# A state-space convolution block: loads of A moved to SP's queue, in-projection moved beside the first convolution, first scan's signs copied from PSUM

## The chip, the cores and the metric

The kernel runs on one core of one Trainium2 chip. The core has five engines with a queue each: TensorE (PE, matrix products into PSUM), VectorE (DVE), ScalarE (ACT), GpSimd (POOL) and SyncE (SP, which here only issues DMAs). DMAs can be issued from SP's queue and from ScalarE's. The metric is the time of one launch in microseconds of the device, the median of several runs, less is better.

## What is computed

The input x has 4 images of 64 x 64 pixels with 96 channels. Layer 0 is a binarised state-space block, layer 1 an attention without softmax and a feed-forward network. What the change touches is all in layer 0:

```python
x = x + conv_block(group_norm(x))
# conv_block, for each image:
xz = sign(x) @ (s_in * sign(W_in - mean)).T + b_in          # in-projection, 96 -> 2 * 192
xp, z = split(xz)
t = conv3x3(sign(xp + move0), scale * sign(conv_W))         # 192 -> 192 channels
t = prelu(t + conv_b + rp_b0) + rp_b1 + xp
xs = silu(t)                                                # in 4 directions: rows, columns, both reversed
dt_r, B, C = split(sign(xs) @ sign(Wl).T * sl + bl)         # 6 + 16 + 16 per direction
delta = softplus(sign(dt_r) @ sign(Wd).T * sd + bd + dt_bias)
A = -exp(A_logs)                                            # 4 x 192 x 16
h[l] = exp(delta[l] * A) * h[l-1] + delta[l] * xs[l] * B[l] # scan along 4096 positions
y[l] = sum_n h[l] * C[l] + D * xs[l]
y = layer_norm(sum over directions(y)) * silu(z)
out = sign(y) @ sign(W_out).T * s_out + b_out
```

Group norm before a sign needs only the mean, so the kernel sums the columns of x and adds the negative group mean before the sign.

## The kernel before

The work falls into a **head** and a long **scan loop**. The scan loop (`Scans.run`) goes through 1536 pieces (4 images, 4 directions, 4 chunks of 1024 positions, 6 groups of 32 channels, 4 quarters of the 16 states; 32 channels by 4 states fill 128 rows). Each piece takes an exponential on ScalarE (`decay`), a product on GpSimd (`inject`), a scan and, in part, a product with C on VectorE, and a reduction on PE. Beside it, a generator `back` brings the later images' preparations and the earlier images' epilogues, one step a piece. The order of instructions is written by hand: generators are advanced in turn by `interleave`, and every engine's queue takes its instructions in the order in which the program wrote them. `Later` holds back stores for some turns and then issues them on SP's queue.

The head prepares image 0 and all constants. `run` interleaves two generators:

- `weights()` (`made`). Up to its first `yield` it issues every load of a weight on SP's queue (L199 to L240), and on ScalarE's queue `pvd` (L241), `sbR` (L245 to L247) and the 24 loads of A (`anm`, L251: 32 rows of 16 single floats each). Then it takes the signs of `w_in` (L259) and transposes them. Its later steps make the convolution's weights and their scales (L265 to L270), the weights of the x projection (L290 to L303), of the delta projection (`wdz`, `wdy`, L314 to L329), then `dbias`, `dsum`, the exponential and negation of A (L336, L337), and many small constants up to L373. It has 22 steps.
- `prologue(c, 0, c.xts)` (`first`). It sums the columns of x on PE (L514, four steps), turns the sums into group means (L521 to L534, three steps), transposes x and takes the signs (`xfin`, eight steps; it also stores x plus the output bias, `xb`). Then comes the in-projection: for both halves h of the channels and all eight q of 512 pixels, two matmuls `px` and `pz` (L562), the sign of px into the padded image `tpad` (L564) and the sign of pz into `sz` (L569), which is stored to DRAM. `alone` is true for this image only.

Then `first` runs the convolution in 16 parts (h, q). A part is 18 matmuls (L616) into one half of the two-bank PSUM tile `cv2`, then v on VectorE (L653) and r on ScalarE (L656) from it, and a matmul `cz` (L658). While the next part's matmuls run in four steps s, the rest of this part is done: two VectorE operations at s = 0, `sign` and an exponential at s = 1, logarithm and exponential at s = 2, the product u at s = 3. The small working tiles come from a pool of eight (`f32`). Part n reads rows of `tpad` that the projections q = n and n + 1 of both halves wrote.

Then the signs are turned into pairs (L685, L690), multiplied (L737), and the six delta inputs of each direction are stored (`sgd`), loaded (`g`, L756), transposed through PE (L761), copied to `gt` (L766), stored (`gTd`, L767) and loaded twice by `load_signs` (L1161, L1162) into the tile `gT`: once at rows 0 to 47, once at rows 64 to 111 and shifted by 16 columns. `gT` feeds the delta matmuls of `prepare` (L1202). The first scan's direction is `KORD[0]` = 1.

```python
made, first = c.weights(), prologue(c, 0, c.xts)
lanes = [made, first]
while (0, 1) not in c.ready:
    interleave(lanes)
    c.later.tick()
```

Of the kernel before, what the change touches and what calls it, by code (L numbers as in the profile page):

```python
# [25 lines left out]
CH = 1024  # L26
# [27 lines left out]
def hybrid_kernel(ctx: ExitStack, tc: tile.TileContext, a: dict, out: bass.AP):  # L54
# [103 lines left out]
    def weights():  # L158
# [89 lines left out]
        for g in range(NG):  # L248
            src = a["al"][32 * (g % 4) : 32 * (g % 4) + 32, g // 4].rearrange("d k (q j) -> j d (k q)", j=4)
            for j in range(4):  # L250
                nc.scalar.dma_start(anm[j::4, g, :], src[j])  # L251
        for t in gTs + [wdz]:
# [82 lines left out]
        nc.vector.tensor_reduce(dsum, pv[:, :, DSK : DSK + NK], AX.X, ALU.add)  # L335
        nc.scalar.activation(anm, anm, AF.Exp)  # L336
        nc.vector.tensor_scalar(anm, anm, -1.0, None, ALU.mult)  # L337
        nc.vector.tensor_reduce(sum4, ident.rearrange("p (d j) -> p d j", j=4), AX.X, ALU.add)
# [94 lines left out]
def run(c):  # L433

    made, first = c.weights(), prologue(c, 0, c.xts)
    lanes = [made, first]
    while (0, 1) not in c.ready:
        interleave(lanes)
        c.later.tick()
# [40 lines left out]
def prologue(c, b, xts=None):  # L480
# [11 lines left out]
    with tc.tile_pool(name=f"xg_{b}", bufs=1) as xgp:  # L492
# [3 lines left out]
        with tc.tile_pool(name=f"cv_{b}", bufs=1) as cvp:  # L496
# [58 lines left out]
            for h in range(2):  # L555
                nc.gpsimd.memset(tflat[h].bitcast(F32), 0.0)
            for h in range(2):
                for q in range(NQ8):
                    cols = slice(512 * q, 512 * q + 512)
                    px, pz = bank(f"ix{h}{q}", 0)[0:96], bank(f"iz{h}{q}", 1)[0:96]  # L560
                    for ps, c0 in ((px, 96 * h), (pz, DN + 96 * h)):
                        nc.tensor.matmul(ps, c.winT[:, c0 : c0 + 96], xsT[:, cols], start=True, stop=True)  # L562
                    yield
                    nc.scalar.activation(  # L564
                        tpad[h][:, 1 + 8 * q : 9 + 8 * q, 1 : 1 + IW], px.rearrange("p (h w) -> p h w", w=IW),
                        AF.Sign, scale=pv[:, h, S_X : S_X + 1], bias=c.sbias[:, h : h + 1], saturate=False,
                    )
                    sz = f32(f"sz{h}{q}").bitcast(BF16)[0:96, 0:512]
                    nc.scalar.activation(  # L569
                        sz, pz, AF.Sign, scale=pv[:, h, S_Z : S_Z + 1], bias=pv[:, h, B_Z : B_Z + 1]  # L570
                    )
                    c.later.store(c.szd[b][h][:, cols], sz)

# [5 lines left out]
            prev = turned = None  # L579
            two = c.p.dA.tile([128, CH], F32, name=f"cv2_{b}", tag="dA") if alone else None  # L580
            utp = sub.enter_context(tc.tile_pool(name=f"ut_{b}", bufs=1))
# [23 lines left out]
            for n, part in enumerate(parts + [None]):  # L605
                if part:
                    h, q = part
                    nm = f"{h}{q}"
                    at = 512 * (n % 2)
                    ps = (two[:, at : at + 512] if alone else bank("cv" + nm, 0))[0:96]  # L610
                for s in range(4 if alone else 5):
                    if part:
                        per = 5 if alone else 4
                        for j, t in taps[per * s : min(18, per * s + per)]:
                            dy, dx = divmod(t, 3)
                            nc.tensor.matmul(  # L616
                                ps, c.cw[:, j, t, 96 * h : 96 * h + 96],
                                tpad[j][:, 8 * q + dy : 8 * q + dy + 8, dx : dx + IW],
                                start=(j == 0 and t == 0), stop=(j == 1 and t == 8),
                            )  # L620
                    if s == 0 and turned:
                        by_columns(*turned)
                        turned = None
# [46 lines left out]
        with tc.tile_pool(name=f"rw_{b}", bufs=1) as rw:  # L670
# [4 lines left out]
            tbg, sgg = (t.rearrange("p (g r) -> p g r", r=64) for t in (tbc, sgn))  # L675
            g2 = rw.tile([128, 2, 320], F8, name=f"g_{b}", tag="g")
            gw = g2.bitcast(F32)
            for o in (1, 0):
# [74 lines left out]
                if o:  # L753
                    nc.gpsimd.memset(gw[:, :, 48:80], 0.0)
                for x, k in enumerate((o, o + 2)):
                    nc.sync.dma_start(gw[:, x, 0:48], c.sgd[b][k].rearrange("(p f) -> p f", p=128))  # L756
                    yield
                    yield
                    gp = bank(f"gp{k}", k // 2).rearrange("p (s f) -> p s f", s=4)
                    for s in range(4):  # L760
                        nc.tensor.matmul(  # L761
                            gp[:, s, :], g2[:, x, 48 * s : 48 * s + 128], c.ident8, start=True, stop=True
                        )
                    yield
                    t = rw.tile([48, 4, 32], F32, name=f"gt_{b}_{k}", tag="gt", bufs=2)
# [362 lines left out]
class Scans:  # L1128
# [6 lines left out]
    def __init__(self, c):  # L1135
# [9 lines left out]
        self.late, self.cys = None, {}  # L1145
        self.us, self.gs, self.at, self.loaded, self.sums = {}, {}, -1, set(), {}

# [213 lines left out]
    def run(self, back):  # L1361
# [4 lines left out]
        for x in range(3):  # L1366
# [5 lines left out]
            )  # L1372
        interleave(lanes)
        for q in range(NQ):
            self.load_bc(0, self.bt, 0, 0, 0, q)
# [125 lines left out]
```

## Time and profile before

| what | us |
|---|---|
| median of 3 runs (5527.49 to 5539.79) | 5532.96 |
| profiled execution, own time | 5528.8 |
| its span, first to last instruction | 5527.0 |
| busy: VectorE | 5025.5 (91%) |
| busy: GpSimd | 4975.1 (90%) |
| busy: ScalarE | 3568.5 (65%) |
| busy: PE, matmuls | 3478.7 (63%) |
| first in-projection matmul (ix) | at 60.14 |
| first convolution matmul | at 84.13 |
| first delta matmul | at 233.01 |
| first injection on GpSimd | at 259.4 |
| first scan on VectorE | at 269.6 |
| mean granted clock of PE | 0.71 of full speed |

Times "at" count from the span's start. Lines of the profile that follow name an engine, a line of the kernel, an operation, and the tiles written and read. A queue such as "SPq" shows the issue of DMAs, not their running. In square brackets stands how long the engine had been idle before, and what released it. In a line of a timeline, several like instructions are merged, "x18" for example.

### The profile page before, as it was taken

How to read it: one execution, taken by the hardware profiler on the slowest of the kernel's cores; microseconds unless marked ns; L12 is line 12 of the kernel's file. 1: busy time of each engine (PE TensorE's matmuls, PEld its weight loads, DVE VectorE, ACT ScalarE, POOL GpSimd, SP SyncE). 2: the span in 40 equal slices, each digit the busy share in tenths (PEclk: the TensorE clock that was granted, in tenths of full speed). 3: DMA queues.
4: the chain of work that ended last, by engine and by line, in shares of the span. 5: the costliest groups of instructions: out<-in, count | busy, mean ns of one | idle time of the engine just before them, and what ended most of it. 6: DMA issues, size and time to landing. Idle time of an engine off the chain costs nothing. (4 is left out here: it accounts for less than half of the span.)

```text
span 5527.0 us, 62184 instructions
## 1 busy us (share of the span) xinstructions
PE 3478.7 (63%) x20133; PEld 1371.3 (25%) x20133; DVE 5025.5 (91%) x3198; ACT 3568.5 (65%) x5568; POOL 4975.1 (90%) x2255
## 2 busy tenths in 40 slices
PE   6456765467645776657665677664677664445677
PEld 2222222122222232222222232221232221111223
DVE  3299999999999999999999999999999999999984
ACT  4467766677666667777666666776556775555554
POOL 2199999899999999999999999999999999999981
PEclk8666776678777776767876777765787565666777
DMA  4455765767666666676765666667666566666652
GB/s 80 120 191 187 211 204 189 237 220 211 200 192 207 197 199 207 195 237 212 223 191 184 206 205 195 198 208 229 201 214 194 179 194 199 213 202 190 204 157 60
DMA packets 613243, 1069.92 MB, mean 194 GB/s; under 512 B 225083, under 2 KB 343924, under 8 KB 611124
## 3 DMA queue, kind: packets, MB, share of 16 engines
q1 hardware_dynamic: 599428, 1065.88, 62.0%
q8 instruction: 158, 2.59, 0.2%
q10 hardware_dynamic: 13488, 0.07, 0.1%
q14 instruction: 169, 1.38, 0.1%
HBM read 833.20 MB, written 229.38 MB: 192 GB/s over the span
## 5 line engine op out<-in xcount | busy, mean ns | idle before, releaser
L404 POOL TENSOR_TENSOR w<-dl,bc 128x1024 f32<-128x1024 f32 x1536 | 3578.8, 2356 | 158.7 <-PE yp L1340 69.6
L1267 ACT ACTIVATE dA<-dl,anm 128x1024 f32<-128x1024 f32 x1536 | 1714.6, 1116 | 495.5 <-DVE w L404 282.7
L404 DVE TENSOR_TENSOR_SCAN dA<-dA,cy,w 128x1024 f32<-128x1024 f32 x711 | 1665.8, 2343 | 98.7 <-ACT dA L1267 94.1
L1340 PE MATMUL yp<-w,sum 128*32 128x256 f32 x12288 | 1289.5, 515 | 401.5 <-POOL w L404 260.0
L404 POOL TENSOR_TENSOR w<-h,bc 128x1024 f32<-128x1024 f32 x587 | 1381.1, 2353 | 114.4 <-DVE h L404 104.2
L404 DVE TENSOR_TENSOR w<-dA,bc 128x1024 f32<-128x1024 f32 x949 | 1162.4, 1225 | 48.7 <-issue 0.9
L404 DVE TENSOR_TENSOR_SCAN h<-dA,cy,w 128x1024 f32<-128x1024 f32 x441 | 1031.6, 2340 | 8.6 <-ACT dA L1267 8.5
L1340 PEld LDWEIGHTS yp<-w,sum 128*32 128x32 f32 x12288 | 316.3, 129 | 1487.4 <-issue 710.4
L1309 ACT COPY cy<-dA 128x1 f32<-128x1 f32 x715 | 112.2, 157 | 747.8 <-DVE w L404 746.2
L404 DVE TENSOR_TENSOR_SCAN dA<-dA,w 128x1024 f32<-128x1024 f32 x238 | 543.3, 2283 | 29.1 <-ACT dA L1267 21.6
L616 PE MATMUL cv<-tp,cw 96*96 96x512 fp8e5 x1152 | 364.4, 452 | 46.2 <-ACT r L656 42.0
L404 DVE TENSOR_TENSOR_SCAN h<-dA,w 128x1024 f32<-128x1024 f32 x146 | 332.5, 2278 | 10.5 <-ACT dA L1267 9.1
L1202 PE MATMUL dps<-gT,wdz 128*128 128x64 fp8e5 x1000 | 113.7, 313 | 339.4 <-ACT ys L1354 310.1
L1215 PE MATMUL dps<-sp,ident 128*128 128x512 f32 x376 | 279.7, 834 | 47.0 <-ACT dps L1211 46.7
L1345 PE MATMUL yp<-ya,back 128*128 128x256 f32 x576 | 239.3, 537 | 1.6 <-DMA ya<-y 1.1
L616 PEld LDWEIGHTS <-cw 96*96 96x96 fp8e5 x1152 | 153.5, 144 | 234.1 <-issue 182.0
L1202 PEld LDWEIGHTS <-wdz 128*128 128x128 fp8e5 x1024 | 95.1, 152 | 427.3 <-issue 395.1
L1202 PE MATMUL dps<-gT,wdy 128*128 128x64 fp8e5 x504 | 59.3, 320 | 204.1 <-ACT ys L1354 202.0
L1309 ACT COPY cy<-h 128x1 f32<-128x1 f32 x437 | 81.4, 186 | 147.5 <-DVE h L404 146.4
L1207 ACT ACTIVATE pd<-dps,dbias,pvd 128x512 f32<-128x512 f32 x188 | 143.2, 761 | 22.6 <-PE dps L1202 22.6
L878 PE MATMUL yc<-eys,mean 96*96 96x512 f32 x240 | 139.2, 734 | 29.2 <-DVE vks L404 13.6
L1345 PEld LDWEIGHTS yp<-ya,back 128*128 128x128 f32 x576 | 123.8, 248 | 130.2 <-issue 93.3
(290 smaller groups left out, 4221.1 us busy)
## 6 DMA issues: line engine op xcount, KB each, us to landing
dl<-dld SPq DMA_DIRECT2D x768, 512.0 KB
bc<-bcd SPq DMA_DIRECT2D x512, 512.0 KB
dld<-pd SPq DMA_DIRECT2D x125, 512.0 KB
yd<-ys SPq DMA_DIRECT2D x768, 64.0 KB
dld<-pd SPq DMA_DIRECT2D x126, 256.0 KB
ya<-yd SPq DMA_DIRECT2D x192, 128.0 KB
pu<-ud SPq DMA_DIRECT2D x32, 512.0 KB
pu<-utd SPq DMA_DIRECT2D x30, 512.0 KB
```

The costliest lines, as they stand in the source:

```text
L404: return getattr(self.eng, name)(out, *args, **kw)
L616: nc.tensor.matmul(ps, c.cw[:, j, t, 96 * h : 96 * h + 96], tpad[j][:, 8 * q + dy : 8 * q + dy + 8, dx : dx + IW], start=(j == 0 and t == ...
L878: self.c.nc.tensor.matmul(ps, w, x, start=(i == 0), stop=(i == len(pairs) - 1))
L1202: nc.tensor.matmul(pv[:, s], wd[:, k, s], gT[:, :, c0 : c0 + 16], start=(s == 0), stop=(s == 7))
L1207: nc.scalar.activation(d[:, 0], ps, AF.Abs, scale=sc, bias=bi)
L1215: nc.tensor.matmul(ps, c.ident, t, start=False, stop=True, skip_group_check=True)
L1267: c.nc.scalar.activation(t, self.dlt[i // NQ][0], AF.Exp, scale=c.anm[:, g, NQ * KORD[e] + q : NQ * KORD[e] + q + 1])
L1309: self.c.nc.scalar.copy(self.carries[g, q], h[:, CH - 1 : CH])
L1340: c.nc.tensor.matmul(y[32 * x : 32 * x + 32, g % 2, :], c.sum4, prod[:, 256 * x : 256 * x + 256], start=(q == 0), stop=(q == NQ - 1 and no ...
L1345: c.nc.tensor.matmul(y[:, g % 2, :], w, src, start=False, stop=(n == len(more) - 1))
```

## The change

1. The 24 loads of A go from ScalarE's queue to SP's. Exponential and negation of A move from `weights()` into `Scans.run`, behind the first round of delta matmuls.
2. `run` advances `made` by one step and `first` by six (column sums and group means), before it interleaves the two.
3. For image 0, the in-projection becomes a list of 16 small generators `project(h, q)`, ordered by q and then h. Four of them run before the convolution. The other twelve run in its parts 0 to 5: matmuls at s = 0 and s = 2, the two signs at s = 1 and s = 3, in each case ahead of the part's other ScalarE work of that step. px and pz now share a second two-bank tile, and `sz` takes the pool `h` of two tiles instead of the pool of eight. The other images do what they did.
4. The tile `g` gets zeros on both sides of its data. For the first direction of image 0, the transposition is done twice, at two offsets, and the two results are copied from PSUM straight into the rows of `gT`. Store and loads of that direction are left out, and `Scans` starts with this tile entered in `gs`.

```diff
--- before.py
+++ after.py
@@ -248,7 +248,7 @@
         for g in range(NG):
             src = a["al"][32 * (g % 4) : 32 * (g % 4) + 32, g // 4].rearrange("d k (q j) -> j d (k q)", j=4)
             for j in range(4):
-                nc.scalar.dma_start(anm[j::4, g, :], src[j])
+                nc.sync.dma_start(anm[j::4, g, :], src[j])
         for t in gTs + [wdz]:
             nc.gpsimd.memset(t.bitcast(F32), 0.0)
 
@@ -333,8 +333,6 @@
                 yield
         nc.vector.tensor_tensor(dbias, pvd[:, :, NK : 2 * NK], pvd[:, :, 2 * NK :], ALU.add)
         nc.vector.tensor_reduce(dsum, pv[:, :, DSK : DSK + NK], AX.X, ALU.add)
-        nc.scalar.activation(anm, anm, AF.Exp)
-        nc.vector.tensor_scalar(anm, anm, -1.0, None, ALU.mult)
         nc.vector.tensor_reduce(sum4, ident.rearrange("p (d j) -> p d j", j=4), AX.X, ALU.add)
         yield
 
@@ -434,6 +432,9 @@
 
     made, first = c.weights(), prologue(c, 0, c.xts)
     lanes = [made, first]
+    next(made)
+    for _ in range(6):
+        next(first)
     while (0, 1) not in c.ready:
         interleave(lanes)
         c.later.tick()
@@ -554,22 +555,41 @@
             nc.gpsimd.memset(xgw[64:128, 1], 0.0)
             for h in range(2):
                 nc.gpsimd.memset(tflat[h].bitcast(F32), 0.0)
-            for h in range(2):
-                for q in range(NQ8):
-                    cols = slice(512 * q, 512 * q + 512)
+            two = [c.p.dA.tile([128, CH], F32, name=f"cv{i}_{b}", tag="dA") for i in range(2)] if alone else None
+
+            def project(h, q):
+
+                cols = slice(512 * q, 512 * q + 512)
+                if alone:
+                    px, pz = two[1][0:96, 0:512], two[1][0:96, 512:CH]
+                else:
                     px, pz = bank(f"ix{h}{q}", 0)[0:96], bank(f"iz{h}{q}", 1)[0:96]
-                    for ps, c0 in ((px, 96 * h), (pz, DN + 96 * h)):
-                        nc.tensor.matmul(ps, c.winT[:, c0 : c0 + 96], xsT[:, cols], start=True, stop=True)
+                for ps, c0 in ((px, 96 * h), (pz, DN + 96 * h)):
+                    nc.tensor.matmul(ps, c.winT[:, c0 : c0 + 96], xsT[:, cols], start=True, stop=True)
+                yield
+                nc.scalar.activation(
+                    tpad[h][:, 1 + 8 * q : 9 + 8 * q, 1 : 1 + IW], px.rearrange("p (h w) -> p h w", w=IW),
+                    AF.Sign, scale=pv[:, h, S_X : S_X + 1], bias=c.sbias[:, h : h + 1], saturate=False,
+                )
+                sz = c.p.h.tile([128, CH], F32, name=f"sz{h}{q}_{b}", tag="h") if alone else f32(f"sz{h}{q}")
+                sz = sz[0:96, 0:256].bitcast(BF16)
+                nc.scalar.activation(
+                    sz, pz, AF.Sign, scale=pv[:, h, S_Z : S_Z + 1], bias=pv[:, h, B_Z : B_Z + 1]
+                )
+                c.later.store(c.szd[b][h][:, cols], sz)
+
+            if alone:
+
+                ahead = [project(h, q) for q in range(NQ8) for h in range(2)]
+                for g in ahead[:4]:
+                    next(g)
                     yield
-                    nc.scalar.activation(
-                        tpad[h][:, 1 + 8 * q : 9 + 8 * q, 1 : 1 + IW], px.rearrange("p (h w) -> p h w", w=IW),
-                        AF.Sign, scale=pv[:, h, S_X : S_X + 1], bias=c.sbias[:, h : h + 1], saturate=False,
-                    )
-                    sz = f32(f"sz{h}{q}").bitcast(BF16)[0:96, 0:512]
-                    nc.scalar.activation(
-                        sz, pz, AF.Sign, scale=pv[:, h, S_Z : S_Z + 1], bias=pv[:, h, B_Z : B_Z + 1]
-                    )
-                    c.later.store(c.szd[b][h][:, cols], sz)
+                    next(g, None)
+                del ahead[:4]
+            else:
+                for h in range(2):
+                    for q in range(NQ8):
+                        yield from project(h, q)
 
 
             yield
@@ -577,7 +597,6 @@
             taps = [(j, t) for j in range(2) for t in range(9)]
             one = lambda h: slice(h, h + 1)
             prev = turned = None
-            two = c.p.dA.tile([128, CH], F32, name=f"cv2_{b}", tag="dA") if alone else None
             utp = sub.enter_context(tc.tile_pool(name=f"ut_{b}", bufs=1))
             uts = {}
 
@@ -607,7 +626,7 @@
                     h, q = part
                     nm = f"{h}{q}"
                     at = 512 * (n % 2)
-                    ps = (two[:, at : at + 512] if alone else bank("cv" + nm, 0))[0:96]
+                    ps = (two[0][:, at : at + 512] if alone else bank("cv" + nm, 0))[0:96]
                 for s in range(4 if alone else 5):
                     if part:
                         per = 5 if alone else 4
@@ -618,6 +637,11 @@
                                 tpad[j][:, 8 * q + dy : 8 * q + dy + 8, dx : dx + IW],
                                 start=(j == 0 and t == 0), stop=(j == 1 and t == 8),
                             )
+                    if alone and ahead:
+                        if s % 2 == 0:
+                            next(ahead[0])
+                        else:
+                            next(ahead.pop(0), None)
                     if s == 0 and turned:
                         by_columns(*turned)
                         turned = None
@@ -673,7 +697,7 @@
             sgw = rw.tile([128, L // 8], F32, name=f"sgn_{b}", tag="sgn")
             sgn = sgw.bitcast(F8)
             tbg, sgg = (t.rearrange("p (g r) -> p g r", r=64) for t in (tbc, sgn))
-            g2 = rw.tile([128, 2, 320], F8, name=f"g_{b}", tag="g")
+            g2 = rw.tile([128, 2, 384], F8, name=f"g_{b}", tag="g")
             gw = g2.bitcast(F32)
             for o in (1, 0):
                 xr = rw.tile([128, 96, 64], BF16, name=f"xr{o}_{b}", tag="xr")
@@ -751,16 +775,29 @@
                     yield
                 c.later.flush()
                 if o:
-                    nc.gpsimd.memset(gw[:, :, 48:80], 0.0)
+                    nc.gpsimd.memset(gw[:, :, 0:16], 0.0)
+                    nc.gpsimd.memset(gw[:, :, 64:96], 0.0)
                 for x, k in enumerate((o, o + 2)):
-                    nc.sync.dma_start(gw[:, x, 0:48], c.sgd[b][k].rearrange("(p f) -> p f", p=128))
+                    nc.sync.dma_start(gw[:, x, 16:64], c.sgd[b][k].rearrange("(p f) -> p f", p=128))
                     yield
                     yield
-                    gp = bank(f"gp{k}", k // 2).rearrange("p (s f) -> p s f", s=4)
-                    for s in range(4):
-                        nc.tensor.matmul(
-                            gp[:, s, :], g2[:, x, 48 * s : 48 * s + 128], c.ident8, start=True, stop=True
+
+                    def columns(j, at):
+                        ps = bank(f"gp{k}{at}", j).rearrange("p (s f) -> p s f", s=4)
+                        for s in range(4):
+                            src = g2[:, x, at + 48 * s : at + 48 * s + 128]
+                            nc.tensor.matmul(ps[:, s, :], src, c.ident8, start=True, stop=True)
+                        return ps
+
+                    gp = columns(k // 2, 64)
+                    if alone and k == KORD[0]:
+
+                        gp2 = columns(1 - k // 2, 0)
+                        nc.scalar.activation(c.gTs[0][0:48], gp[0:48], AF.Copy, saturate=False)
+                        nc.scalar.activation(
+                            c.gTs[0][64:112, :, 0:112], gp2[64:112, :, 16:128], AF.Copy, saturate=False
                         )
+                        continue
                     yield
                     t = rw.tile([48, 4, 32], F32, name=f"gt_{b}_{k}", tag="gt", bufs=2)
                     nc.scalar.activation(t.bitcast(F8), gp[0:48], AF.Copy, saturate=False)
@@ -1143,7 +1180,8 @@
         ]
         self.bt, self.ct, self.dlt, self.ins, self.dAs, self.carries, self.ydone = {}, {}, {}, {}, {}, {}, {}
         self.late, self.cys = None, {}
-        self.us, self.gs, self.at, self.loaded, self.sums = {}, {}, -1, set(), {}
+        self.gs = {(0, KORD[0]): c.gTs[0]}
+        self.us, self.at, self.loaded, self.sums = {}, -1, set(), {}
 
     def done(self, b, n):
 
@@ -1371,6 +1409,8 @@
                 ))
             )
         interleave(lanes)
+        c.nc.scalar.activation(c.anm, c.anm, AF.Exp)
+        c.nc.vector.tensor_scalar(c.anm, c.anm, -1.0, None, ALU.mult)
         for q in range(NQ):
             self.load_bc(0, self.bt, 0, 0, 0, q)
             self.load_bc(1, self.ct, 0, 0, 0, q)
```

## What the change was forecast to do

> **What bounds the kernel now.** I read the page first, then busy time by stage, then the timeline of the first 270 us, then what SP's queue waits for.
>
> ```profile
> span 5527.0 us, 62184 instructions
> DVE  3299999999999999999999999999999999999984
> POOL 2199999899999999999999999999999999999981
> ```
>
> From the third of 40 slices on, VectorE and GpSimd are full. The stages show it in numbers (columns: stretch, length, then busy us of PE, weight load, VectorE, ScalarE, GpSimd):
>
> ```profile
> 0.00:84.00 84.00, 41.32 (x191) 19.10 (x192) 25.28 (x69) 40.35 (x70) 23.97 (x87) 0.82 0.58 98
> 84.00:190.00 106.00, 77.15 (x305) 40.24 (x303) 47.98 (x64) 50.91 (x82) 16.17 (x16) 0.90 0.29 60
> 270.00:5450.00 5180.00, 3274.81 (x19239) 1267.29 (x19239) 4911.49 (x2989) 3406.10 (x5302) 4923.53 (x2147) 0.71 0.64 200
> ```
>
> In the 5180 us of the scan loop both engines are 95% busy (4911 and 4924), and the diff leaves the order of that loop as it is. So the change can only move the loop's start: the first injection on GpSimd at 259.4, the first scan on VectorE at 269.6. I take every us by which the head is shortened as a us of the end. The head is three stages: loads and weights to 84, convolution to 190, the scan inputs to 270.
>
> Loads (start, length, queue, source; "Aq" is an engine's DMA queue):
>
> ```profile
> 12.15 18.28 ACTq L251 DMA_DIRECT2D anm<-in_al  x24
> 30.48 0.91 ACT L259 ACTIVATE slab<-slab,slab 128x96 bf16<-128x96 f32 x3 [28.46 <-DMA anm<-in_al]
> ...
> 53.49 0.30 SPq L240 DMA_DIRECT2D bff<-in_bff  x1
> 53.89 7.67 SPq L423 DMA_DIRECT2D xbd<-xb  x8
> 62.59 22.89 SPq L423 DMA_DIRECT2D szd<-sz  x16
> ```
> ```profile
> SPq L206 <- DMA anm<-in_al: 10.8, 5, 3.8
> ```
>
> ScalarE computes nothing until 30.48, because its queue issues the 24 loads of A. They also hold SP, for 10.8 us in five waits (view of SP's own waits). SP needs until 53.8 for the weights' loads.
>
> One part of the convolution, of 16:
>
> ```profile
> 97.35 4.08 PE L616 MATMUL cv<-tp,cw 96*96 96x512 fp8e5 x18 [1.49 <-ACT r L656]
> 98.24 0.59 ACT L597 ACTIVATE sg<-cz 96x512 fp8e5<-96x512 f32 x1 [0.94 <-DVE cz L404]
> ...
> 100.67 0.69 DVE L404 TENSOR_TENSOR u<-cz,e 96x512 f32<-96x512 f32 x1 [2.47 <-ACT e L640]
> 101.47 0.81 DVE L653 TENSOR_SCALAR v<-cv,acs,acb 96x512 f32<-96x512 f32 x1
> 102.32 0.77 ACT L656 ACTIVATE r<-cv,cbias,csc 96x512 f32<-96x512 f32 x1 [1.68 <-DVE v L653]
> ```
>
> It is a ring: 18 matmuls, v on VectorE, r on ScalarE, and the next part's matmuls wait for r though they write the tile's other half. 4.08 + 0.81 + 0.77 and the steps between make 5.79 us. Later every second part takes 7.45, because PE runs part of it at half clock. Parts 0, 1, 2 and 6 start at 84.13, 91.56, 97.35 and 120.63.
>
> Signs of the first scan:
>
> ```profile
> 226.13 0.59 ACT L766 ACTIVATE gt<-gp 48x512 fp8e5<-48x512 f32 x1 [4.70 <-PE gp L761]
> 230.54 0.37 SPq L1161 DMA_DIRECT2D gT<-gTd  x1
> 233.01 1.86 PE L1202 MATMUL dA_s<-gT,wdz 128*128 128x64 fp8e5 x16 [3.10 <-DMA gT<-gTd]
> ```
>
> **What the Trainium skill says.** "DMA: Bandwidth & Descriptors", section "Issuing engines are not separate DMA queues": transfers started by different engines run on the same 16 DMA engines, so a second queue saves issue time only. The trace agrees for A (SP's 10.8 us). The same page, "Rules for kernel authors": a non-contiguous last dimension becomes one descriptor per element. A's loads are such: 24 of 2 KB cost 0.643 us of issue each (median), against 0.31 for a 192 KB store of xb. "TensorE: Matmul & The Clock Gate", Part 1: PE falls to half clock after a window of about 3.4 us with little work. The trace has the two speeds (18 taps in 4.08 or 5.75 us). The same page, "Architectural detail": ScalarE and VectorE are strict FIFO, which the ring above shows too.
>
> **The change, part by part.**
>
> *A onto SP, column sums first.* ScalarE is free at about 12. The signs of w_in can run at 13.5, and column sums (7.45 us of PE), their transposes and gsum end near 25 instead of 45. SP loses its 10.8 us of waits, so the last weight load (bff) is issued near 42.8. But then the 24 loads of A come, 24 x (0.643 + 0.05) = 16.6, to 59.4, and all stores of the head queue behind them: 8 of xb, 8 x 0.37 = 3.0, to 62.4, then the first of sz. With one lead of five steps `first` would reach its fourth projection near 54 (weights' steps 48.6 to 55.5 of the trace, minus about 5 of alignment and some of the load gain). There the new sz tiles stop it: the pool `h` has two, so the third sz waits until the first is stored. Queued on ScalarE behind that wait are the fourth tp and everything after; PE waits too, since the fourth px overwrites the bank pair that sz reads. The first store lands at about 66.8: a small store's issue at 221.46 released its load at 223.71, so 2.25 us, and 1.57 MB of xb lie in front of it (4.4 us at the 357 GB/s seen at 240 to 250). Then sz 0.76, px and pz about 1: first taps near 69.3 instead of 84.13, **-14.8**. Most of what ScalarE and the column sums gain is hidden behind SP. Bounds: if A's loads take 0.30 on SP (the cheapest issue in the trace) it is 8 us earlier, at 0.80 (their slowest) 4 later.
>
> *In-projection beside the convolution.* 12 of 16 projections move into parts 0 to 5, two a part, each with 2 matmuls and two ScalarE instructions (0.78 and 0.77, one every 0.66). ScalarE's order in a part becomes tp, sz, sg, e, Ln, Exp, tp, sz, r. From a part's first tap: 5 taps and px, pz on PE to 1.73 (1.13 + 0.43 + 0.17); tp 1.78, sz 2.44, sg 3.10, e 3.59, Ln 4.21, Exp 4.87 to 5.50; u on VectorE to 6.23, v to 7.10; r 7.15 to 7.92. The second tp and sz (5.53 to 6.95) fit beside u and v. So 8.0 us instead of 5.79, and PE idles 2.6 us of it instead of 1.5: the slow clock will hit the first five taps more often. It costs 0 to 1.3 us (1.56 us of PE work doubled); I take 0.4, so 8.4. Bounds 7.6 (tp not waiting for pz) and 9.3.
> Parts 0 and 1 also carry the tail of the weights, which now comes behind the fourth projection: three batches of 8 transposes, three casts of 1.22, and the 6.6 us of small VectorE work that ran beside the projections at 64.6 to 71.3. Followed through PE's and VectorE's order, part 0 takes 12.1 (7.43 before) and part 1 9.6 (5.79). Part 1 starts near 81.4, part 2 near 91.0, part 6 at 91.0 + 4 x 8.4 = 124.6: **+4.0** against 120.63, all gains before it included. Parts 6 to 15 stay, ± 5 for how the slow windows fall (five of ten parts have one, 1.66 each).
>
> *Signs from the bank.* Gone: one store, two loads of gT, and the second direction's wait behind that store on SP. Added: 4 matmuls (0.6) and a second copy of at most 0.59. The first gp is ready at 225.49; both copies end near 227.3. The second direction's gp needs that bank and runs to 228.0, then 4 transposes of the next part (0.63): first dps matmul at 228.6 instead of 233.01, -4.4. The 8 loads of bc (4 MB, near 12 us) start only 2.9 earlier, so between 2.9 and 4.4 is left; I take **-4.0**. Exp and negation of A move to where ScalarE waits for these matmuls (0.31 and 0.20): nothing, at worst 0.5. The wider g tile: nothing.
>
> Sum: +4.0 - 4.0 = **0**. The profiled execution took 5528.8 (span 5527.0 and 1.8 around it), 4.2 below the median of 5532.96; a difference of nothing leaves the median.
>
> **The rivals.**
> 1. *The trade is even* (forecast): 5533, own range 5524 to 5543.
> 2. *SP doesn't hold the third sz*: A's loads go out at 0.3 each, or SP gains more than 10.8 from an emptier queue. First taps at 55 to 61, the weights' tail then partly runs in the projections' shadow again. 8 to 14 off, and parts 2 to 5 at 8.0 (1.6 off): 5518. For it: contention stretched every wait of SP before 31 us. Against: A's issue time hardly varies (606 to 801 ns), also where SP waited.
> 3. *Slower, by PE's clock*: the 2.6 us of idle PE in parts 1 to 5 bring the slow clock into each part's first taps and keep it in step for parts 6 to 15. Five parts at 9.7 (+6.5), five more long ones later (+8.3): 5548. It decides from about 9.2 us a part with nine of the last ten slow. For it: a gap of 1.5 already slows every second part. Against: parts 1 to 4 before had that gap and stayed fast.
> 4. *The short cut of the signs does little*, since the loads of bc set when dl can land: 5535.
>
> **How the numbers follow.** Chances: 62%, 24%, 8%, 6%. About 0.2% (11 us) is what a measurement of this kernel can tell from no change. Faster by more: four fifths of rival 2 and a little of the first, 0.23. Slower: rival 3 and the first's upper edge, 0.11. Same: 0.66. The range goes from rival 2's middle to the forecast's upper edge, 5517 to 5543.
>
> **What would show it.** In the changed trace: `anm` on SP from about 43 to 59; the third L569-like sz waiting for a DMA of szd until about 67; first taps near 69; parts 1 to 5 at 8 to 9 us with r last behind v; part 6 within 5 us of 120.6; no store of gTd for the first direction and the first dps matmul about 4 us earlier in its stage. If sz never waits and taps begin before 61, rival 2 is right. If the loop's length (259.4 to the end) changes by more than 5 us, my premise that only its start moves is wrong.

## The result and the profile after

The changed kernel took 5533.78 us (median of 4 runs, 5533.03 to 5535.9) against 5531.23 of the kernel before on the same chip; the ratio is 1.0003, with a 95% interval of 0.9986 to 1.002. A second comparison, with more runs, gave 5529.94 against 5530.94, ratio 0.9995 (0.9987 to 1.0004). No difference can be told, as forecast. The profiled execution took 5535.9, its span 5534.1.

From the page of the changed kernel, the two engines that bound the loop, in 40 slices:

```profile
DVE  3299999999999999999999999999999999999984
POOL 2199999899999999999999999999999999999981
```

Busy time by stage, changed kernel (stretch, length, then PE, weight load, VectorE, ScalarE, GpSimd, granted clock, DMA share, GB/s):

```profile
0.00:84.00 84.00, 40.54 (x212) 22.62 (x213) 27.45 (x71) 30.34 (x55) 24.03 (x87) 0.76 0.57 90
84.00:190.00 106.00, 75.46 (x284) 38.86 (x282) 44.63 (x60) 58.11 (x93) 15.79 (x15) 0.89 0.31 66
270.00:5450.00 5180.00, 3270.83 (x19202) 1256.47 (x19201) 4908.91 (x2985) 3402.81 (x5296) 4923.71 (x2149) 0.71 0.63 200
```

VectorE and GpSimd are as busy in the loop as before, to 3 us. What changed is where ScalarE works: 10 us less in the first 84, 7 more in the convolution. ScalarE is indeed free early, and the column sums come early; its own timeline has the line that ends them, at 23.82:

```profile
23.82 0.15 ACT L530 COPY cs<-cst 96x1 f32<-96x1 f32 x1 [0.92 <-PE cst L525]
```

But what it gained is waited away again (timeline of all engines, changed kernel; start, length, and in brackets the idle time and its releaser):

```profile
41.91 17.21 SPq L251 DMA_DIRECT2D anm<-in_al  x24
...
59.65 4.25 SPq L421 DMA_DIRECT2D xbd<-xb  x8
...
63.99 6.42 SPq L421 DMA_DIRECT2D szd<-sz  x4
...
66.77 0.77 ACT L576 ACTIVATE sz<-cv,pv 96x512 bf16<-96x512 f32 x1 [14.57 <-DMA szd<-sz]
...
69.25 2.01 PE L635 MATMUL cv<-tp,cw 96*96 96x512 fp8e5 x5
```

Read it from below: the first taps (69.25) stand behind a projection that waited for sz; ScalarE waited 14.57 us for the first store of sz, since sz has only two tiles; that store was issued at 63.99, because SP issued A from 41.91 to 59.1 and then, from 59.65, the eight stores of xb. All of it is one queue.

The end of part 4 (first tap at 105.16) and of part 5, with two projections in each:

```profile
110.70 0.69 DVE L402 TENSOR_TENSOR u<-cz,e 96x512 f32<-96x512 f32 x1 [4.68 <-ACT e L664]
111.18 0.76 ACT L576 ACTIVATE sz<-cv,pv 96x512 bf16<-96x512 f32 x1
111.31 0.80 DVE L677 TENSOR_SCALAR v<-cv,acs,acb 96x512 f32<-96x512 f32 x1
...
112.14 0.77 ACT L680 ACTIVATE r<-cv,cbias,csc 96x512 f32<-96x512 f32 x1 [0.20 <-DVE v L677]
...
112.53 0.61 SPq L421 DMA_DIRECT2D utd<-ut  x1
112.97 1.25 PE L635 MATMUL cv<-tp,cw 96*96 96x512 fp8e5 x5 [2.64 <-ACT r L680]
...
113.24 6.04 SPq L421 DMA_DIRECT2D szd<-sz  x1
...
121.06 0.77 ACT L576 ACTIVATE sz<-cv,pv 96x512 bf16<-96x512 f32 x1 [1.97 <-DMA szd<-sz]
```

In part 4, PE waits 2.64 us for r at the end. VectorE waited 4.68 us for the exponential, so u is late, v behind it in the same queue, r behind v. In part 5 sz waits once more for a tile: from 113.24 on, SP's issue of one store of sz took 6.04 us, behind `utd`, the store of the turned u.

And the signs of the first direction, which now go from the bank (changed kernel):

```profile
229.24 0.59 ACT L796 ACTIVATE gT<-gp 48x512 fp8e5<-48x512 f32 x1 [4.59 <-PE gp L789]
...
231.25 1.91 PE L1240 MATMUL dA_s<-gT,wdz 128*128 128x64 fp8e5 x16
```

### The profile page after: what moved, and what is told of

Read it like the earlier page. It is cut to its first block, busy times and chain, and to the rows that moved or that the text cites. A ratio compares the mean times of both kernels' runs of the same rounds, so it can differ in the third digit from the quotient of the medians.

```text
span 5534.1 us, 62174 instructions
## 1 busy us (share of the span) xinstructions
PE 3479.7 (63%) x20137; PEld 1368.2 (25%) x20137; DVE 5024.8 (91%) x3198; ACT 3568.1 (64%) x5569; POOL 4975.6 (90%) x2259
## 5 line engine op out<-in xcount | busy, mean ns | idle before, releaser
L402 DVE TENSOR_TENSOR_SCAN dA<-dA,cy,w 128x1024 f32<-128x1024 f32 x711 | 1665.8, 2343 | 99.1 <-ACT dA L1305 89.6
L402 DVE TENSOR_TENSOR_SCAN h<-dA,w 128x1024 f32<-128x1024 f32 x146 | 332.5, 2278 | 11.1 <-ACT dA L1305 8.9
L1383 PEld LDWEIGHTS yp<-ya,back 128*128 128x128 f32 x576 | 123.3, 247 | 130.9 <-issue 94.7
```

Source lines behind the costliest of these rows:

```text
L402: return getattr(self.eng, name)(out, *args, **kw)
L1383: c.nc.tensor.matmul(y[:, g % 2, :], w, src, start=False, stop=(n == len(more) - 1))
```

## The experiments

Marks of all profiles, in us from the start of the span. "Long" counts the parts 6 to 14 that took 7.4 us or more instead of 5.8. "Loop" is the start of the last of 1536 scans minus that of the first. Times are medians; each ratio is to runs of the kernel before on the same chip.

| run | first taps | part 6 | long | first scan | loop | time | ratio (95%) |
|---|---|---|---|---|---|---|---|
| before | 84.1 | 120.6 | 4 | 269.6 | 5135.2 | 5531.23 | |
| before_again | 83.8 | 120.3 | 4 | 269.5 | 5137.0 | 5528.66 (one run) | |
| changed | 69.3 | 122.5 | 4 | 269.0 | 5144.3 | 5533.78 | 1.0003 (0.9986 to 1.002) |
| after_again | 71.0 | 127.2 | 3 | 271.2 | 5135.6 | 5529.94 | 0.9995 (0.9987 to 1.0004) |
| a_late | 56.5 | 109.1 | 1 | 249.3 | 5139.7 | 5513.08 | 0.9963 (0.995 to 0.9976) |
| sz_free | 52.9 | 109.3 | 3 | 254.2 | 5136.8 | 5517.62 (one run) | |
| a_act | 70.8 | 123.3 | 2 | 265.9 | 5132.3 | 5527.60 | 0.9991 (0.9984 to 0.9997) |
| order | 71.0 | 115.0 | 4 | 260.7 | 5139.9 | 5525.12 | 0.9989 (0.9982 to 0.9996) |
| proj_first | 86.6 | 125.2 | 3 | 269.1 | 5138.9 | 5531.71 | 0.9998 (0.9989 to 1.0006) |
| no_bank | 70.0 | 122.8 | 3 | 270.3 | 5129.3 | 5523.74 (one run) | |
| best | 56.3 | 100.7 | 2 | 243.8 | 5138.5 | 5506.56 | 0.9951 (0.9936 to 0.9965) |
| warm | 55.5 | 99.1 | 1 | 241.0 | 5139.5 | 5505.86 (one run) | |
| final | 58.2 | 101.8 | 2 | 245.4 | 5134.1 | 5505.82 | 0.9955 (0.9941 to 0.9969) |
| warm_before | 84.4 | 122.2 | 0 | 264.4 | 5136.1 | 5523.82 | 0.999 (0.9983 to 0.9996) |

The loop's length scatters over 15 us with no relation to the edit. So single times can't be compared closely; the marks of the head can, to some 2 us (5 at part 6 of the changed kernel).

**Is it A on SP's queue? (a_late)** The loads are collected in `weights()` and issued later, in the convolution:

```diff
-                nc.sync.dma_start(anm[j::4, g, :], src[j])
+                a_loads.append((anm[j::4, g, :], src[j]))
...
                     prev = (h, q, pz, v, r, nm)
+                    if alone and 6 <= n < 14:
+                        for _ in range(3):
+                            nc.sync.dma_start(*c.a_loads.pop(0))
```

> All of the change, but the 24 loads of A are issued on SP three a part in parts 6 to 13 of the convolution, not ahead of the head's stores. Theory (SP's queue in front of the sz stores is what holds the third sz, so the 24 x 0.72 us of A are the price): third sz runs near 50 to 53 instead of 66.8, first taps at 54 to 58 instead of 69.25, part 6 11 to 14 us earlier than 122.55 (at 109 to 112), whole time 11 to 14 below the changed kernel. Rival (the tail of the weights and the ring of ScalarE and PE take the place of the wait): first taps may come early, but part 6 not more than 3 us earlier, and the time the same.

Timeline of a_late:

```profile
54.06 0.76 ACT L578 ACTIVATE sz<-cv,pv 96x512 bf16<-96x512 f32 x1
...
56.54 2.04 PE L637 MATMUL cv<-tp,cw 96*96 96x512 fp8e5 x5
```

The third sz runs at 54.06 and waits for no store; first taps at 56.5, part 6 at 109.1, 13.4 earlier: inside the theory's bounds, but for sz, which is 1 us late. (A shorter stop of 4.39 us appeared at the last xb, which by the profile waits for a store of xb. Why stays open.) The first scan is 19.8 earlier, more than expected: from part 6 on a_late had one long part and the changed kernel four. The time is 0.37% below the kernel before; by the two ratios of the changed kernel that is some 18 to 22 us below it, more than the expected 11 to 14.

**Is it the tile? (sz_free)** A stays ahead on SP; the first four sz take tiles of a pool that is idle then:

```diff
-                sz = c.p.h.tile([128, CH], F32, name=f"sz{h}{q}_{b}", tag="h") if alone else f32(f"sz{h}{q}")
+                if alone:
+                    pool, tag = (c.p.w, "w") if q < 2 else (c.p.h, "h")
+                    sz = pool.tile([128, CH], F32, name=f"sz{h}{q}_{b}", tag=tag)
+                else:
+                    sz = f32(f"sz{h}{q}")
```

> All of the change, A on SP in its old place; only the first four sz tiles come from a pool of nine that is idle then, so the third sz waits for no store. Theory (it is the wait for a tile, not the traffic of A's loads or the weights' tail, that stops the third sz): sz doesn't wait, first taps at 54 to 58 as without A's loads; but parts 0 to 5 need tiles from the pool of two again, so the fifth sz may then wait for the stores behind A, until about 67. Rival (tile was not what it waited for): first taps stay at 67 to 69.

Timeline of sz_free:

```profile
44.72 16.26 SPq L251 DMA_DIRECT2D anm<-in_al  x24
...
52.88 2.06 PE L639 MATMUL cv<-tp,cw 96*96 96x512 fp8e5 x5
...
63.68 0.81 DVE L681 TENSOR_SCALAR v<-cv,acs,acb 96x512 f32<-96x512 f32 x1 [2.34 <-DMA xbd<-xb]
```

With the 24 loads still in front, the third sz runs at 50.41 and taps begin at 52.9, a little before the expected 54, while SP is half way through A. So at this place neither A's traffic nor its data mattered, only the tile that had to be stored first. Parts 0 and 1 then took 12.5 and 10.4 us, against 10.0 and 8.1 in a_late. The expected second stop of sz, in part 1, is only 1.10 us. But the last line shows the same wait at another tile: v of part 0 waits 2.34 us for a store of xb, which stands behind A (SP issues the eight of them from 61.51), and r, behind v, 3.81. How much of the difference this makes was not taken apart. Part 6 came at 109.3, as in a_late.

**Would A have been better left on ScalarE? (a_act)** L251 alone goes back to `nc.scalar`.

> All of the change, but the 24 loads of A stay on ScalarE's queue. Theory (it doesn't matter whose queue issues A, as long as it is ahead of the sz stores: on ScalarE it holds SP's weights' loads by about 11 us, on SP it takes 17 us itself; and a_late has shown what is to be had without either): last weight load near 53.8, xb stores to about 62, third sz freed at 65 to 67, first taps at 66 to 69, part 6 within 4 us of the changed kernel's 122.55, the time the same as the changed kernel's. Rival (moving A is the part of the change that pays, since ScalarE is free from 12 instead of 30): first taps after 74, part 6 at 128 or later, the time 5 us or more above the changed kernel.

What SP waited for until 60 us, in a_act (total, times, longest):

```profile
SPq L206 <- DMA anm<-in_al: 11.1, 5, 4.6
```

ScalarE's timeline, same run:

```profile
40.47 0.15 ACT L530 COPY cs<-cst 96x1 f32<-96x1 f32 x1 [0.92 <-PE cst L525]
...
68.35 0.76 ACT L576 ACTIVATE sz<-cv,pv 96x512 bf16<-96x512 f32 x1
```

First taps 70.8 and part 6 123.3 are within 1.6 us of the changed kernel, and the first scan (265.9) is even earlier, so moving A bought nothing here. The theory had part 6 and the time right, the first taps 1.8 past its range, and the way wrong: the third sz (68.35) doesn't wait for a store. The sums are late (40.47 against 23.82), and with them the last xb (61.03 against 44.50) and everything behind. On ScalarE's queue A costs the start of the work; on SP's it costs the end.

**What sets the length of parts 0 to 5? (order)** The projections' matmuls go to s = 1 and s = 3, tp and sz behind the exponential and behind r:

```diff
-                    if alone and ahead:
-                        if s % 2 == 0:
-                            next(ahead[0])
-                        else:
-                            next(ahead.pop(0), None)
+                    if alone and ahead and s % 2:
+                        next(ahead[0])
...
+                    if alone and ahead and s == 2:
+                        next(ahead.pop(0), None)
                     yield
...
                     prev = (h, q, pz, v, r, nm)
+                    if alone and ahead:
+                        next(ahead.pop(0), None)
```

> All of the change; in parts 0 to 5 the matmuls of the two projections go to s = 1 and s = 3, the first tp and sz behind logarithm and exponential of s = 2, the second tp and sz behind r. Theory (tp and sz stand ahead of sg, e, Ln and Exp on ScalarE and so put u, v and r late; the part's length is that chain): parts 1 to 5 take 6.3 to 7.3 us each instead of 7.8 to 9.6, first taps stay at 69, part 6 is 6 to 11 us earlier, the time 6 to 11 below the changed kernel. Rival (PE, with its slow clock, or the ScalarE total sets the part): parts stay at 8 or more, and part 6 within 2 us of 122.5.

The end of part 3 in the timeline of order (first tap at 96.12):

```profile
100.18 0.69 DVE L402 TENSOR_TENSOR u<-cz,e 96x512 f32<-96x512 f32 x1 [2.52 <-ACT e L661]
...
102.45 2.34 PE L635 MATMUL cv<-tp,cw 96*96 96x512 fp8e5 x10 [0.17 <-ACT r L679]
```

u starts 4.06 us after the first tap instead of 5.54, and PE waits 0.17 at the end instead of 2.64. Parts 2 to 5 take 6.3 us each, with the same work in them as in the changed kernel, so neither PE's nor ScalarE's total sets the part. (The edit moves the projections' matmuls by a step as well; which of the two moves counts was not separated.) Part 1 missed the expected figure (8.5): the tail of the weights runs in it too. Part 6 came 7.6 earlier than in the first profile of the changed kernel, the first scan 8.3. The times say less: by the ratios order is 3 to 8 us below the changed kernel, and its interval overlaps those of both comparisons.

**Does the overlap itself save? (proj_first)** The list `ahead` stays empty, the 16 projections run before the convolution with banks and pool as before:

```diff
-                ahead = [project(h, q) for q in range(NQ8) for h in range(2)]
...
+            ahead = []
+            for h in range(2):
+                for q in range(NQ8):
+                    yield from project(h, q)
```

> All of the change, but the in-projection is its own stage ahead of the convolution, as before. Theory (parts 0 to 5 at 8.5 us with two projections in them against 5.8 alone give back what the shorter stage ahead saves): sz tiles come from the pool of eight, so projections begin at about 44 and stop at the ninth sz until xb and the first szd are stored, near 66; the stage then takes 23 to 27 us as before, first taps at 78 to 86, part 6 at 115 to 123 and the time within 4 us of the changed kernel. Rival (the overlap itself saves): part 6 at 127 or later.

Timeline of proj_first:

```profile
63.79 0.78 ACT L573 ACTIVATE sz<-iz,pv 96x512 bf16<-96x512 f32 x1 [17.11 <-DMA xbd<-xb]
```

Part 6 at 125.2 lies between what the two theories allowed, so it decides nothing; the first scan (269.1 against 269.0) and the time do: the overlap, in the order in which it was written, saves nothing. (First taps at 86.6 are 0.6 past the expected range.) The stop merely moves: here it is the first sz, not the ninth as I had expected, since the eight tiles of its pool hold xb until xb is stored, which again waits behind A.

**What is the short cut of the signs worth? (no_bank)** The branch `if alone and k == KORD[0]` is taken out and `gs` begins empty.

> All of the change, but the first scan's signs are stored and loaded as before. Theory (the short cut brings 4.0 of the 4.0 us that the head wins back): measured from the end of the convolution (first xa), the first delta matmul comes 4.4 to 5.0 us later than in the changed kernel (its distance there is 38.0, before 43.0), the first injection 3.0 to 4.0 later, the first scan 3 to 4 later. Rival (the loads of bc set it anyway): the delta matmul is later, the injection and the scan within 1 us of the changed kernel.

Timeline of no_bank:

```profile
233.42 1.86 PE L1232 MATMUL dA_s<-gT,wdz 128*128 128x64 fp8e5 x16 [3.17 <-DMA gT<-gTd]
```

From xa (190.44) to the first delta matmul it takes 42.98 us; with the short cut 38.02 (193.23 to 231.25) and 37.95 in the second profile. From xa to the first injection 69.3 against 66.3, to the first scan 79.9 against 75.8 and 76.4. So 5.0 us are won, and 3.0 to 4.1 are left at the loop's start, not next to nothing, as the rival had it. Where the rest goes can be read from SP's waits between 244 and 258 us (changed kernel, then no_bank):

```profile
SPq L1282 <- DMA dld<-w_s: 4.4, 1, 4.4
SPq L1274 <- DMA dld<-w_s: 2.5, 1, 2.5
```

The store of delta (`dld`) is issued 4.9 us earlier, but SP then waits 1.9 longer for it before the first load `dl` can go. The DMA engines are 0.9 to 1.0 busy from 240 to 252 us, with the loads of bc among others; that these hold the store is likely, but no run shows it.

**Both edits together (best).** a_late and order in one kernel.

> The changed kernel with both edits, A's loads in parts 6 to 13 and the order of tp and sz in parts 0 to 5 (a_late and order together). If the two prices add up: first taps at 56 to 58, parts 2 to 5 at 6.3, part 6 at 100 to 103 against 122.55, first scan 26 to 29 us earlier than the changed kernel's 269.04, time 22 to 29 below it. If they cover one another (the tail of the weights then sets parts 0 to 2): part 6 at 106 to 109, time as a_late.

They add up, almost: part 6 at 100.7, first scan 25.3 earlier than the changed kernel's 269.0 (19.8 and 8.3 alone); the time is 0.49% below the kernel before, which is 27 us (19 to 35).

**What are the long parts? (warm, warm_before, final)** Into PE's gap at the end of a part go five matmuls whose result nobody reads, in warm and final (on best; final is warm's kernel, timed) from part 6 on, in warm_before (on the kernel before) in all parts. The edit of warm_before, without the line that makes the tile `idle`:

```diff
                     prev = (h, q, pz, v, r, nm)
+                    if alone:
+                        for _ in range(5):
+                            nc.tensor.matmul(idle[0:96, 0:512], c.winT[:, 0:96], xsT[:, 0:512], start=True, stop=True)
```

> best, with five matmuls more in each part from 6 on, behind cz, into the tile of px and pz, which nobody reads then (1.06 us of PE in its gap of 1.5). Theory (the parts of 7.5 us are PE's half clock, which follows from the gap): all ten parts 6 to 15 take 5.8 to 5.9. Rival (the slow parts come from elsewhere, or five matmuls more make the ring longer): as many parts at 7.5 as in best, or all parts 6.3 and more.

> The kernel before, with five matmuls more in each part of the convolution, behind cz, into an idle tile of PSUM (1.06 us in PE's gap of 1.5). Theory (the parts of 7.45 us are PE's half clock, called by its idle gap): all 16 parts at 5.8 to 5.9, where before had six at 7.4 to 7.5; first scan 8 to 10 us earlier (near 260), time 8 to 10 below. Rival (slow parts have another cause, or they merely fall differently in each kernel): four or more parts of 7.4 stay, or the parts become 6.3 and longer.

> The kernel of the run warm, timed: first scan near 241, that is 28 us earlier than the changed kernel's, part 7 and later at 5.8, time 25 to 31 below the changed kernel and 1 to 4 below best.

The taps of one part in the timeline of warm_before:

```profile
104.71 4.08 PE L616 MATMUL cv<-tp,cw 96*96 96x512 fp8e5 x18 [0.41 <-ACT r L656]
```

PE waits 0.41 us a part instead of 1.5, the ring stays at 5.8, and no part behind part 0 (8.7) is long any more. The granted clock is the column before the last two; first the kernel before, from its first tap to its last part:

```profile
84.13:179.60 95.47, 72.72 (x286) 38.04 (x285) 43.47 (x58) 45.31 (x73) 14.71 (x14) 0.91 0.31 64
```

then warm_before:

```profile
84.40:174.60 90.20, 83.58 (x362) 45.30 (x361) 43.53 (x58) 45.34 (x73) 14.86 (x14) 0.97 0.32 66
```

More work on PE, a higher clock, 5.3 us less time: in this kernel the long parts follow from the gap. The first scan came 5.2 earlier, less than the 8 to 10 expected: there were four long parts to win, not five or six (4 x 1.66 = 6.6), and part 0 grew by 1.3.

On best it decides nothing: best has just two long parts of its own, 6 and 7. Ahead of part 6 no matmul was added; part 7 was short in warm and long in final, which stays open. The time of final is that of best, not 1 to 4 below it, and its first scan is at 245.4, not near 241.

That a_late and best have so few long parts goes together with the size of the gap. The kernel before, taps of parts 5 to 7, then the stretch with the gap ahead of part 6 and the next one:

```profile
114.78 4.08 PE L616 MATMUL cv<-tp,cw 96*96 96x512 fp8e5 x18 [1.55 <-ACT r L656]
120.63 5.75 PE L616 MATMUL cv<-tp,cw 96*96 96x512 fp8e5 x18 [1.55 <-ACT r L656]
128.09 4.08 PE L616 MATMUL cv<-tp,cw 96*96 96x512 fp8e5 x18 [1.49 <-ACT r L656]
```
```profile
117.96:121.37 3.41, 1.86 (x10) 0.94 (x8) 2.88 (x4) 0.89 (x2) 0.00 (x0) 1.00 0.89 129
121.37:124.79 3.42, 3.42 (x10) 1.61 (x9) 0.81 (x2) 2.34 (x4) 1.09 (x2) 0.50 0.46 131
```

The long part holds one stretch of 3.42 us at half clock, and half of that is about the 1.66 us by which it is longer (an estimate from these lines). The gaps come in two sizes. In parts 7 to 14 of the eleven profiles without added matmuls, the gap ahead of a part is 1.49 us in 54 of them, and none is long; it is 1.54 or 1.55 in 32, and 23 are long; in the other two it is over 3 us, and both are long. In a_late and best, six of the seven gaps ahead of parts 8 to 14 are of 1.49. That the 0.06 us decide, and what makes a gap 1.49 or 1.55, no run tested.

**Is the loop longer? (before_again, after_again)** Both kernels without an edit.

> The kernel before, profiled once more. Theory (the scan loop's 7 us between the two profiles is what executions differ by anyway): first injection within 1 us of 259.4 and first scan within 1 us of 269.6, but the last scan's start differs from the first profile's 5404.75 by several us. Rival (the changed kernel makes the loop longer): the last scan's start within 2 us of 5404.75.

> The changed kernel, once more. If the 7 us by which its loop was longer in its first profile are what executions differ by: part 6 within 2 us of 122.55, first scan within 2 us of 269.04, and a loop from first to last scan of 5132 to 5140 us instead of 5144.3. If the change makes the loop longer: 5143 or more again. The time is within 4 us of the kernel before in either case.

The kernel before repeats its first scan within 0.1 us, and its loop within 1.9; the last scan starts 1.8 us from the first profile's, which by the terms of that run speaks for the rival. The second profile of the changed kernel decides: a loop of 5135.6 instead of 5144.3. So the 9 us between the loops of the first two profiles were the execution's, not the kernel's. Its head doesn't repeat as closely as expected: part 6 at 127.2 instead of 122.5, first scan 2.2 later.

## Why the forecast was right

- **A on SP.** Forecast: issued from 43 to 59, 16.6 us. Measured 41.91 to 59.1, 17.21; SP's 10.8 us of waits for A gone. The Trainium skill ("DMA: Bandwidth & Descriptors", "Issuing engines are not separate DMA queues") says that a second queue saves issue time only. Here SP saves not even that: what A costs SP in waits from ScalarE's queue (11.1 us in a_act), it costs SP in issue from its own (17.2).
- **The third sz.** Forecast: freed at 66.8, first taps at 69.3. Measured 66.77 and 69.25, and 68.55 and 71.03 in the second profile. a_late and sz_free show the cause from both ends: without A in front, or with another tile, the stop goes. That the figure is exact is luck: the store was issued at 63.99, not at 62.4, and freed its tile 2.8 us later, not 4.4, since the stores of xb had been on their way from 59.65 on.
- **Parts 0 and 1.** Forecast 21.7 us together, measured 18.5 and 21.4.
- **Parts 2 to 5.** Forecast 8.4 each, of which 8.0 by ScalarE's order and 0.4 for the slow clock. Part 4 without a long stretch took 7.81, with u from 5.54 to 6.23 after the first tap, the very figure of the forecast. Parts 2 to 4 took 9.1, 8.3 and 7.8, and in the second profile 7.7, 9.6 and 7.8: a mean of 8.4 both times. order shows that it is indeed the place of the projections in the part, and not their work.
- **Missed: part 5's sz** waits 1.97 us for a store, because SP's next issue behind `utd` (issued at 112.53) took 6.04. With r behind it, part 5 takes 9.6 and 9.5. The forecast knew of the two tiles; it did not look at what else stands in SP's queue there. It cost some 1.2 us against the 8.4.
- **At xa, the end of the convolution,** the changed kernel is 3.2 and 5.1 us later than before in two pairs of profiles; the forecast was 4.0 later.
- **The signs.** Forecast -4.4 at the delta matmul and -4.0 at the scan; by no_bank -5.0 and -3.4 to -4.1. The loads of bc start 2.9 earlier, as forecast.
- **Sum.** Forecast 0; the first scan is 0.6 earlier in one pair of profiles and 1.7 later in the other. The whole time alone would prove little: ten of the fourteen times in the table lie within the forecast's 5517 to 5543. It is the marks of the head that bear the forecast out.
- **The rivals.** Rival 2 (SP doesn't hold sz) didn't come; a_late and sz_free build its outcome, at 5513 and 5517.6. Its own sum, 8 to 14 and 1.6 off, gives 5517 to 5523, so 5518 is its fast end and not its middle. Rival 3 (the slow clock in step) didn't come: three or four long parts of nine, as before (four there, not the five that the prediction counted); that a gap of PE can bring the slow clock, warm_before shows. The fast parts 2 to 4 before, named against it, had gaps of 1.49. Rival 4 falls with no_bank.
- **The stated alarm went off falsely.** From the first injection to the end, the two first profiles differ by 6.9 us, above my 5 (by 9.2 from first to last scan). A bound taken from one profile of each kernel was too tight: 14 profiles of a loop that no edit touched lie between 5129.3 and 5144.3.

So the expected gain of the change is there, and is spent in its own second half: the first taps come 15 us earlier, parts 0 to 5 take it back, and the signs' 3 to 4 us pay for what they take beyond that. a_late and order remove the two causes, and best keeps the gain of both.

## What to carry to other kernels

Moving the loads of A from a compute engine's queue to one that computes nothing paid nothing here, because stores that others needed were queued behind them: look at what the new queue has to issue next, and put loads that are needed late late. Put work beside a ring behind the ring's own instructions in the queues that it shares; here the same instructions cost 2 us a part in front and 0.5 behind. And a wait for "the store" is often a wait for a tile: four tiles of an idle pool brought part 6 as far forward as moving 24 loads out of the way (109.3 and 109.1).

## What the runs showed of the hardware

One store, `utd` (768 KB), holds up the next issue on its queue. It issues in 0.61 us itself, but whatever SP issues next takes 5.98 to 6.11 us, four times in the head of all 14 profiles: 6.04 (sz, changed), 6.03 (ud, before), 6.07 (A, a_late). The DMA view of the changed kernel from 110 to 122 us:

```profile
DMA packets 6687, 1.25 MB, mean 104 GB/s; under 512 B 6272, under 2 KB 6591, under 8 KB 6687
```

Nearly all packets of that stretch are below 512 bytes; that their number is what holds the queue is a guess that no run tried.

Filling most of a gap of 1.5 us on PE with matmuls for nothing made the real ones faster: 4.08 us behind part 0 in every part, instead of 5.75 in four of them, at a granted clock of 0.97 instead of 0.91. Without such matmuls no part from 7 to 14 behind a gap of 1.49 us was slow, and 23 of 32 behind 1.54 or 1.55 were.
